# A decoder with two layers: one of three general PSUM banks becomes two halves for the attention units' transposed words, and four weights of the writing order change

## The chip, the core and the metric

The kernel is one program on one core of a Trainium2 chip. The metric is the device time of one execution in microseconds (us), from its start to its last store; less is better. Five engines take part, each working through its own list of instructions in order: PE (TensorE: matmuls and transposes, which write to PSUM), DVE (VectorE), ACT (ScalarE), POOL (GpSimd) and SP (which here issues most DMA transfers). Engines wait for each other by semaphores. An instruction that waits holds up everything behind it on its own engine.

## The reference, cut to what matters

The input x has 4 batches of 256 rows of 256 numbers, 1024 rows in all. Six blocks are added to it in turn, each on a layer norm of the rows: a linear attention with decay, four experts chosen by token, a layer that looks up 64 of 2048 small experts for each row, a convolution with attention inside blocks of 16 rows, a cross attention with quantised operands, and a layer of 16 experts of which each row uses two, beside a shared one. The change sits in the fifth block:

```
q = (x @ Wq + bq).reshape(1, B * N, H, hd)            # 1024 rows, 16 heads of 16
kv = (cond @ Wkv + bkv).reshape(1, -1, 2, H, hd)      # 1024 keys and values
q = _fq_sym(q, axis=-1); k = _fq_sym(k, axis=-1); v = _fq_sym(v, axis=2)
attn = jnp.einsum('bhqd,bhkd->bhqk', q, k)
attn = jax.nn.softmax(attn, axis=-1)
attn = _fq_unsigned(attn, axis=-1)                    # rounded to 255 steps of the row's maximum
out = jnp.einsum('bhqk,bhkd->bhqd', attn, v)          # then out @ Wp + bp
```

## The kernel before, in words

The 1024 rows are eight tiles (t = 0 to 7) of 128 rows. The cross attention is worked in 128 **units**, one for a tile and a head, by `units(k, n)` in six lanes. A unit does this:

1. PE writes the scores of 128 rows against 1024 keys into one of two score buffers, `sc0` and `sc1`, which are as large as two banks each (two matmuls `sc<-kT,qT`).
2. DVE takes the row's extreme from them (`junk<-sc,dsq,nsq`, result `nb`).
3. ACT takes the exponential, rounds it to bytes `e` and sums it; then the score buffer is given back.
4. PE transposes `e`, read as words of four bytes: two transposes `f<-ident,e` into half a PSUM bank `tp`.
5. ACT or DVE copies `tp` back over `e` (`e<-f`); then the bank is given back.
6. POOL turns the bytes into bf16 (`qqT<-e`), and PE multiplies them with the values in eight small matmuls into `accs`.

When the 16 heads of a tile are through, `cross_out` divides, transposes and projects them (`ident,ao`, `w_wp,aoT`) and adds them to the tile. `routes` then does the layer norm, the gate and the ranking of that tile, `shared` its shared expert. The tiles form two groups, 0 to 4 and 5 to 7. When a group's last tile is routed, `plan(g)` works out which rows each expert gets (its small matmuls are `ident_,ohs`). Then POOL fetches the rows of each expert tile from DRAM by an indirect DMA (`xr<-xs,smap`) and `routed` works on it: transposes `ident,xr`, two matmuls with the expert's weights (`w,xrT`), ACT and DVE, transposes `ident,rhd`, and two matmuls with `rhT`. Group 0 has 15 such tiles in two lanes beside the units (`beside`), group 1 has 12 in four lanes at the end (`ending`). `combine` fetches the results and adds them to the rows.

**PSUM.** `both`/`accs` takes one tile of 2 KB per partition, and seven more, `f0` to `f6`, are handed out by `bank`, an object of the class `Banks`: `take` gives the one that came free first, `give` returns it. Before the units begin, `turn` takes `f3` to `f6` out (`bank.leave(passed)`) and lays the two score buffers in their place, so that for the time of the units three general banks, `f0` to `f2`, are left. From these three come the words of all units and everything of `local_attention`, `cross_out`, `routes`, `shared`, `plan` and `routed`. When the last unit is done, `ending` closes the score buffers and gives four banks back.

**The order.** Nothing is scheduled by the tool: the order of instructions on each engine is the order in which the Python program writes them. Each strand of work is a generator that yields before each step, naming the engine that it needs next. `Clock.weave` keeps an estimated time for each engine (class `Clock`, `note`: a cost for each kind of instruction) and continues the strand that could start first, where each strand's start is moved ahead by its `lead` and ties go by its `rank`. So a lead, a rank or the number of free banks decides the order, and changes it everywhere behind. Every engine instruction is issued from one helper line, 81, so the rows of the profile are told apart by their tiles and not by their lines.

Of the kernel before, what the change touches and what calls it, by code (L numbers as in the profile page):

```python
# [21 lines left out]
P = 128  # L22
# [163 lines left out]
class Banks:  # L186
# [9 lines left out]
    def take(self, shape, dtype=F32):  # L196
        while not self.free:
            yield "tensor", self.ready()
        item = min(self.free, key=self.free.get)
        self.clock.t = max(self.clock.t, self.free.pop(item))  # L200
        pool, tag = item
        t = pool.tile(shape, dtype, name=tag.rstrip("0123456789"), tag=tag)
        self.held[id(t)] = item, t
        return t

# [39 lines left out]
def decoder(ctx, tc, a, out):  # L245
# [3 lines left out]
    ck = Clock(nc)  # L249
# [11 lines left out]
    A = SimpleNamespace(turned=None, scored=None, folded=None, cleared=[], spare=[], planned={}, mapped={}, loaded=None)  # L261
    wa = front_ctx.enter_context(tc.tile_pool(name="wa", bufs=1, side="right"))

    def load(pool, name, shape, view=None, dtype=F32):
        s = pool.tile(shape, dtype, name="w_" + name, tag="w_" + name)
        nc.sync.dma_start(s, a[name] if view is None else view)
        return s
# [30 lines left out]
    keys = load(wa, "keys", [P, 8, 2 * NKEY])  # L298
# [51 lines left out]
    psf = bank_ctx.enter_context(tc.tile_pool(name="psf", bufs=1, space=PSUM))  # L350
    kept, passed = [(psp, f"f{i}") for i in range(3)], [(psf, f"f{i}") for i in range(3, 7)]
    bank = Banks(ck, kept + passed)

    both = psp.tile([P, 2, D], F32, name="accs", tag="accs")
    accs = [both[:, i] for i in range(2)]
# [438 lines left out]
    def blend():  # L794

        for b in range(NB):
            yield "tensor", lambda: summed.get(("w", b))
            ww = wide["w", b]
            acc = yield from bank.several(2, [P, D])
            for i in range(2):  # L800
                for n in range(PN // 2):
                    te_.matmul(acc[i], ww[:, i, n, :], M.ut[:, n, :], start=(n == 0), stop=(n == PN // 2 - 1))
            summed["m", b] = ck.end
            yield "vector", None
            for i in range(2):
                t = 2 * b + i
                ve_.tensor_tensor(xt[t], acc[i], xt[t], ALU.add)
                bank.give(acc[i])
                added[t] = ck.end
            yield "vector", None  # L810
# [104 lines left out]
    def turn():  # L915
# [68 lines left out]
        mix_ctx.close()  # L984
        A.ps = score_ctx.enter_context(tc.tile_pool(name="ps", bufs=1, space=PSUM))
        A.sc = Banks(ck, [(A.ps, "sc0"), (A.ps, "sc1")])
        wd = late_ctx.enter_context(tc.tile_pool(name="wd", bufs=1))
        A.rt = late_ctx.enter_context(tc.tile_pool(name="rt", bufs=1))
        A.re = late_ctx.enter_context(tc.tile_pool(name="re", bufs=1))
# [193 lines left out]
    def units(k, n):  # L1183

        work = A.late
        for j in range(k, NT * XH, n):
            t, h = j // XH, j % XH
            yield "tensor", lambda: qready.get(t)
            o, c = h % 2, h // 2
            psc = yield from A.sc.take([P, T])  # L1190
            for n_ in range(2):
                te_.matmul(psc[:, n_ * 512:(n_ + 1) * 512], QT[t][:, o, c, :], KV.kT[:, c, n_ * 512:(n_ + 1) * 512],
                           start=True, stop=True)
            yield "vector", None
            nb = work.tile([P, 1], F32, name="nb", tag=f"nb{k}")
            ve_.tensor_tensor_reduce(A.junk, psc, DSQ[t][:, h:h + 1].to_broadcast([P, T]), NSQ[t][:, h:h + 1], 3.0e38,
                                     ALU.add, ALU.min, accum_out=nb)
            yield "scalar", None

            e = work.tile([P, T], U8, name="e", tag=f"e{k}")  # L1200
            se_.activation(e, psc, AF.Exp, bias=nb, scale=SQ[t][:, h:h + 1], accum_out=SUMS[t][:, h:h + 1])
            A.sc.give(psc)
            yield "tensor", None

            tp = yield from bank.take([P, 2, P])
            for o in range(2):
                te_.transpose(tp[:, o, :], e.bitcast(F32)[:, o * P:(o + 1) * P], ident)
            yield "either", None
            words = e.bitcast(I32).rearrange("p (o q) -> p o q", o=2)
            ck.leave(words, tp.bitcast(I32))  # L1210
            bank.give(tp)
            yield "gpsimd", None
            qqT = work.tile([P, 8, P], BF16, name="qqT", tag=f"qqT{k}")
            ge_.tensor_copy(qqT.rearrange("p (o j) q -> p o j q", o=2), words.bitcast(U8).rearrange("p o (q j) -> p o j q", j=4))

            yield "tensor", lambda: 0.0 if t < 2 else summed.get(("o", t - 2))
            for s in range(NT):
                te_.matmul(accs[t % 2][:, h * XD:(h + 1) * XD], qqT[:, s, :], KV.vi[:, s, h * XD:(h + 1) * XD],
                           start=False, stop=(s == NT - 1), skip_group_check=True)
            nunits[t] += 1  # L1220
            if nunits[t] == XH:
                summed[("x", t)] = ck.end
# [203 lines left out]
    def fetch_rows(g, i, xr):  # L1426

        ge_.indirect_dma_start(out=xr, out_offset=None, in_=xs[g],
                               in_offset=bass.IndirectOffsetOnAxis(ap=A.smap[g][:, i:i + 1], axis=0))
# [56 lines left out]
    def ending():  # L1486

        g = NG - 1
        yield "gpsimd", lambda: summed.get(("o", NT - 1))
        unit_ctx.close()  # L1490
        A.fin = fin_ctx.enter_context(tc.tile_pool(name="fin", bufs=1))
        score_ctx.close()
        pse = psum_ctx.enter_context(tc.tile_pool(name="pse", bufs=1, space=PSUM))
        for i in range(4):
            bank.free[pse, f"f{3 + i}"] = ck.end
        yield "gpsimd", lambda: A.mapped.get(g)
        got = {}

        def lane(k):
            for i in range(k, MOST[g], 4):  # L1500
                yield "tensor", lambda: got[i][1] if i in got else None
                yield from routed(g, i, A.fin, f"e{k}", *got[i])

        for i in range(MOST[g]):
            xr = A.fin.tile([P, D], F32, name="xr", tag=f"xre{i}")
            fetch_rows(g, i, xr)
            got[i] = xr, ck.end + 3.0
            if i < 4:
                ck.begin(lane(i))
            yield "gpsimd", None  # L1510
# [31 lines left out]
    def follow(b):  # L1542

        if b >= 2:
            yield "vector", lambda: known.get(b - 2)
        yield from front(b)

    def after_turn(gen, *args):
        yield "vector", lambda: A.scored
        yield from gen(*args)  # L1550

    with tc.manual_schedule(engines={mybir.EngineType.PE, mybir.EngineType.Activation, mybir.EngineType.DVE, mybir.EngineType.Pool}):
        lead = dict(front=(1.85, 0.2, 0.22, 0.3), begin=(0.0, 5.0, 10.0, 80.0), keys=1.2, dense=0.85,
                    blend=-0.82, mixing=(0.6, 0.53), local=(0.7, 0.6), units=0.66, out=0.77, shared=0.13,
                    route=0.66, ending=0.7, combine=0.3, routed=0.71, turn=0.1)
        rank = dict(front=(0, 9, 2, 4), keys=7, dense=1, blend=7, mixing=(5, 8), local=(7, 6), units=3,
                    out=4, routed=8, shared=9, route=2, turn=0, ending=2, combine=1)
        one = lambda k, i=None: (lead[k], rank[k]) if i is None else (lead[k][i], rank[k][i])
        ck.weave([*[Stream(follow(b), one("front", b), lead["begin"][b]) for b in range(NB)],
                  Stream(keys_values(), one("keys")), Stream(dense(), one("dense")), Stream(blend(), one("blend")),  # L1560
                  *[Stream(mixing(k, 2), one("mixing", k)) for k in range(2)],
                  Stream(tables(), one("turn")), Stream(turn(), one("turn")),
                  *[Stream(locals_(k), one("local", k)) for k in range(2)],
                  *[Stream(after_turn(units, k, UN), one("units")) for k in range(UN)],
                  Stream(cross_out(), one("out")), Stream(routes(), one("route")), Stream(shared(), one("shared")),
                  *[Stream(beside(k, 2), one("routed")) for k in range(2)],
                  Stream(ending(), one("ending")), Stream(combine(), one("combine"))])
# [6 lines left out]
    with tc.If(extra > 0, preferred_fallthrough_block=False):  # L1574
        for g, ts in enumerate(GROUPS):
            for i in range(MOST[g], NSL[g]):
# [4 lines left out]
                tp = ps.tile([P, 2, P], F32, name="tp", tag="tp")  # L1581
# [12 lines left out]
                tp = ps.tile([P, 2, P], F32, name="tp", tag="tp")  # L1594
# [18 lines left out]
            for i, t in enumerate(ts):  # L1613
                for j in range(2):
                    yg = work.tile([P, D], F32, name="yg", tag="yg")
                    nc.gpsimd.indirect_dma_start(
                        out=yg, out_offset=None, in_=ys[g],
# [83 lines left out]
```

## Time and profile before

| | us |
|---|---|
| three runs | 1013.13, 1009.01, 1011.62; median 1011.62 |
| the profiled execution | 1012.24 (its span 1010.5, so 1.7 lie around it) |
| before the units (0 to 577) | 577 |
| the units (577 to 913) | 336 |
| what follows the last unit (913 to the end) | 98 |

The three stretches are read from the times at which the first and the last unit's instructions start in the trace: the exponential of the first unit starts at 577.46, the last transposes of words at 911.45. Busy times of the whole span:

| engine | busy us | share |
|---|---|---|
| PE | 755.7 | 75% |
| DVE | 784.2 | 78% |
| ACT | 465.8 | 46% |
| POOL | 329.8 | 33% |

In rows of the profile "out<-in" are the tiles written and read, "x128" is a count, "idle before" is the time for which the engine stood still just before, and "<-" is what ended that. In a table by stage, each engine's busy time is followed by the number of its instructions, then come the granted PE clock, the busy share of the DMA engines and their GB/s.

### The profile page before, as it was taken

Reading aid. Unit: us, or ns where it says so; the run is one execution under the profiler, and the core shown is the slowest. Engines: PE = TensorE matmul, PEld = TensorE weight load, DVE = VectorE, ACT = ScalarE, POOL = GpSimd, SP = SyncE. Lnnn points to the kernel's source line nnn. Section 1 sums busy time; section 2 is a strip of 40 time slices with the busy share of each in tenths; the row PEclk is TensorE's granted clock in tenths of the full one; section 3 lists DMA queues with packets and bytes.
Section 4 is the critical chain, followed back from the end, with each engine's and each line's share of the span. In section 5 each row is a group of like instructions: output and inputs, shape, how many; then the busy total and the mean of one; then the engine's idle time right before and its main releaser. Section 6 shows DMA issues by size and latency. Waiting matters only on the chain.

```text
span 1010.5 us, 19521 instructions
## 1 busy us (share of the span) xinstructions
PE 755.7 (75%) x7395; PEld 572.9 (57%) x7430; DVE 784.2 (78%) x2121; ACT 465.8 (46%) x989; POOL 329.8 (33%) x298
## 2 busy tenths in 40 slices
PE   4587953879979798783888577876777768888693
PEld 3465652768768686773666454644455445554451
DVE  4668579898989897999677378889999788875343
ACT  2232440546226332430643177577768766753130
POOL 2000021351042304505511344334444445552522
PEclk9799995999979898796999889969898687999796
DMA  7000050000000001201000610000000290111323
GB/s 249 22 21 21 22 146 22 22 2 3 22 22 2 2 12 33 73 3 61 4 2 2 220 35 3 6 1 6 6 2 6 87 263 21 44 47 47 84 90 96
DMA packets 33938, 46.26 MB, mean 46 GB/s; under 512 B 6096, under 2 KB 25040, under 8 KB 33584
## 3 DMA queue, kind: packets, MB, share of 16 engines
q1 hardware_dynamic: 31776, 39.31, 12.6%
q0 software_dynamic: 2064, 5.64, 2.3%
q8 instruction: 61, 1.00, 0.4%
q14 instruction: 37, 0.30, 0.1%
HBM read 33.87 MB, written 11.08 MB: 44 GB/s over the span
## 4 chain that ended last, share of the span: by engine, by line
DVE 41%; PE 39%; ACT 8%; issue 6%; DMA 3%; POOL 1%; another core or an unknown queue 1%; SPq 0%; POOLq 0%; ACTq 0%; DVEq 0%
PE f L81 36%; DVE junk L81 7%; ACT e L81 5%; DVE aa L81 3%; PE sc L81 3%; DVE mi L81 2%; DVE rden L81 2%; DVE parts L81 2%; DVE jj L81 1%; DVE wq L81 1%; DVE at L81 1%; DVE oh L81 1%; DVE x L81 1%; DVE pk L81 1%; DVE f L81 1%
## 5 line engine op out<-in xcount | busy, mean ns | idle before, releaser
L81 POOL CAST qqT<-e 128x1024 bf16<-128x1024 uint8 x128 | 133.4, 1053 | 165.7 <-ACT e L81 129.6
L81 ACT ACTIVATE e<-sc,nb,qs_q 128x1024 uint8<-128x1024 f32 x128 | 153.9, 1203 | 47.3 <-DVE nb L81 44.2
L81 DVE CUSTOM_DVE_ANT_0 junk<-sc,dsq,nsq 128x1024 bf16<-128x1024 f32 x128 | 163.4, 1276 | 14.1 <-PE sc L81 5.8
L81 PE MATMUL sc<-kT,qT 128*128 128x512 bf16 x221 | 82.8, 449 | 68.3 <-ACT e L81 66.1
L81 POOL TENSOR_SCALAR at<-idx,row 128x512 f32<-128x512 uint8 x32 | 64.8, 2034 | 137.9 <-DMA idx<-mdram 100.7
L81 POOL TENSOR_TENSOR ln_rstd<-ln_ve,mhalf 128x2 f32<-128x2 f32 (+1 forms) x28 | 22.6, 807 | 198.9 <-DVE ln_ve L81 121.8
L81 PEld LDWEIGHTS <-qT 128*128 128x128 bf16 x256 | 23.9, 103 | 82.3 <-issue 78.4
L81 POOL TENSOR_TENSOR parts<-jj,wq 64x1024 f32<-64x1024 f32 x16 | 40.9, 2553 | 80.2 <-DVE wq L81 75.5
L81 PE MATMUL f<-ident,e 128*128 128x128 f32 x256 | 60.2, 323 | 8.1 <-ACT e L81 3.1
L81 PE MATMUL f<-zt,at 128*64 128x64 f32 x1024 | 46.1, 252 | 22.2 <-DVE at L81 19.9
L81 PEld LDWEIGHTS <-qqT 128*128 128x128 bf16 x1024 | 45.5, 101 | 23.5 <-issue 9.8
L81 PEld LDWEIGHTS f<-zt,at 128*64 128x64 f32 x1024 | 41.7, 163 | 29.6 <-issue 19.9
L81 ACT COPY ww<-f 64x256 f32<-64x256 f32 x128 | 46.9, 366 | 24.5 <-PE f L81 23.0
L81 PE MATMUL f<-w_ut,ww 128*128 128x256 f32 x256 | 56.0, 379 | 0.0
L81 PEld LDWEIGHTS f<-ident,e 128*128 128x128 f32 x256 | 37.5, 164 | 30.3 <-issue 10.3
L81 ACT ACTIVATE ln_xn<-x,ln_nmr,ln_rstd 128x256 f32<-128x256 f32 x48 | 27.0, 594 | 55.2 <-DVE ln_nmr L81 53.1
L81 PEld LDWEIGHTS f<-w_ut,ww 128*128 128x128 f32 x256 | 48.6, 190 | 6.6
L81 ACT COPY e<-f 128x256 int32<-128x256 int32 x106 | 38.7, 369 | 28.8 <-PE f L81 27.6
L81 PE MATMUL accs<-vi,qqT 128*128 128x16 bf16 x1024 | 45.5, 172 | 5.2 <-POOL qqT L81 3.3
L81 PE MATMUL f<-w,xrT 128*128 x108 | 40.1, 507 | 7.6 <-DVE xrT L81 7.0
L81 ACT COPY zt<-f 64x512 f32<-64x512 f32 x64 | 37.1, 580 | 18.3 <-PE f L81 17.4
L81 PE MATMUL f<-parts,aa 128*64 128x64 f32 x1024 | 36.6, 235 | 6.5 <-POOL parts L81 3.2
(317 smaller groups left out, 1823.8 us busy)
## 6 DMA issues: line engine op xcount, KB each, us to landing
w<-in_w SPq DMA_DIRECT2D x1, 5632.0 KB
idx<-mdram SPq DMA_DIRECT2D x32, 128.0 KB, 2.9
ys<-ryr SPq DMA_DIRECT2D x27, 128.0 KB, 1.7
kdram<-kb SPq DMA_DIRECT2D x4, 512.0 KB, 4.4
w_ut<-in_ut SPq DMA_DIRECT2D x2, 1024.0 KB, 11.8
kT<-kdram SPq DMA_DIRECT2D x8, 256.0 KB, 5.9
w_w2a<-in_w SPq DMA_DIRECT2D x1, 2048.0 KB, 26.9
ys<-zero SPq DMA_DIRECT2D x1, 1408.0 KB, 7.2
```

Of the source, the lines that this page charges most:

```text
L81: return emit(*args, **kw)
```

## The change

The half bank that a unit's words need no longer comes from the three general banks. `turn` takes one of them for good as `A.pair`, 128 partitions by 2 by 256 numbers, and makes its two halves the free items of a second `Banks` object, `half`. Units take and give halves, everything else has the other two banks. `ending` gives the pair back to `bank` once the last unit is through. Besides, three leads and a rank change: `out`, `routed` and `turn` (the lead of the strands `tables` and `turn`), and the rank of the units.

```diff
@@ Banks.take
-        t = pool.tile(shape, dtype, name=tag.rstrip("0123456789"), tag=tag)
+        if isinstance(tag, int):
+            t = self.tile[:, tag]
+            if len(shape) == 3:
+                t = t.rearrange("p (a b) -> p a b", b=shape[2])
+        else:
+            t = pool.tile(shape, dtype, name=tag.rstrip("0123456789"), tag=tag)
@@ decoder
     bank = Banks(ck, kept + passed)
+    half = Banks(ck, [])
@@ turn, after the score buffers are laid out
         A.sc = Banks(ck, [(A.ps, "sc0"), (A.ps, "sc1")])
+        A.pair = yield from bank.take([P, 2, 256])
+        for i in range(2):
+            half.free["half", i] = ck.end
+        half.tile = A.pair
@@ units
-            tp = yield from bank.take([P, 2, P])
+            tp = yield from half.take([P, 2, P])
...
-            bank.give(tp)
+            half.give(tp)
@@ ending
             bank.free[pse, f"f{3 + i}"] = ck.end
+        bank.give(A.pair)
@@ the weights
-                    blend=-0.82, mixing=(0.6, 0.53), local=(0.7, 0.6), units=0.66, out=0.77, shared=0.13,
-                    route=0.66, ending=0.7, combine=0.3, routed=0.71, turn=0.1)
-        rank = dict(front=(0, 9, 2, 4), keys=7, dense=1, blend=7, mixing=(5, 8), local=(7, 6), units=3,
+                    blend=-0.82, mixing=(0.6, 0.53), local=(0.7, 0.6), units=0.66, out=1.75, shared=0.13,
+                    route=0.66, ending=0.7, combine=0.3, routed=0.81, turn=-0.4)
+        rank = dict(front=(0, 9, 2, 4), keys=7, dense=1, blend=7, mixing=(5, 8), local=(7, 6), units=4,
```

Of the arithmetic nothing changes: every engine instruction is written as before, but on some of them ACT and DVE change places, since `Clock.leave` gives a copy out of PSUM to whichever of the two it reckons free first.

## The prediction

> **What bounds the kernel now.** I read the page first (the span, and busy shares of 75% for PE and 78% for DVE, so no engine bounds the whole), then a table by stage, and then, stage by stage, groups, waits and the order of time.
>
> ```profile
> span 1010.5 us, 19521 instructions
> ```
>
> ```profile
> core 0: us, PE busy (x) PEld busy (x) DVE busy (x) ACT busy (x) POOL busy (x), PEclk, DMA share, GB/s
> 470.00:577.00 107.00, 84.97 (x1187) 69.12 (x1189) 69.02 (x146) 38.97 (x89) 39.51 (x41) 0.93 0.14 44
> 577.00:913.00 336.00, 252.80 (x2259) 169.48 (x2292) 286.93 (x659) 234.72 (x476) 150.18 (x150) 0.86 0.15 44
> ...
> 913.00:980.00 67.00, 55.52 (x218) 33.03 (x217) 30.79 (x124) 17.86 (x60) 24.13 (x26) 0.90 0.29 78
> ```
>
> In the units' 336 us DVE is busy for 287, or 85%; ACT for 70%. Behind the last unit PE takes over (55.5 of 67 us). The groups and waits of the units' stage alone:
>
> ```profile
> L81 DVE CUSTOM_DVE_ANT_0 junk<-sc,dsq,nsq 128x1024 bf16<-128x1024 f32 x128 | 163.4, 1276 | 14.1 <-PE sc L81 5.8 <-remote 2.4 <-PE f L81 1.3
> L81 ACT ACTIVATE e<-sc,nb,qs_q 128x1024 uint8<-128x1024 f32 x128 | 153.9, 1203 | 47.3 <-DVE nb L81 44.2 <-DVE sw L81 0.5
> ...
> L81 PE MATMUL f<-ident,e 128*128 128x128 f32 x256 | 60.2, 323 | 8.1 <-ACT e L81 3.1 <-DVE qT L81 1.7 <-issue 1.2
> ...
> L81 ACT COPY e<-f 128x256 int32<-128x256 int32 x106 | 38.7, 369 | 28.8 <-PE f L81 27.6
> ...
> L81 DVE COPY e<-f 128x256 int32<-128x256 int32 x22 | 9.2, 420 | 0.9 <-PE f L81 0.9
> ```
>
> ```profile
> PE sc L81 <- ACT e L81: 66.1, 67, 9.3
> ACT e L81 <- DVE nb L81: 44.2, 53, 7.3
> ACT e L81 <- PE f L81: 27.6, 42, 1.7
> ```
>
> DVE's row maximum hardly waits (14.1 us over 128 units). ACT waits for DVE, and PE for ACT to free a score buffer. So the chain runs in turn over DVE, ACT and PE, with DVE the fullest. The third row of the groups is the one that the change is about: in front of all 256 transposes of words PE stood still for 8.1 us, and not all of that was for a bank.
>
> At the end the order of time shows what the last group waits for:
>
> ```profile
> 935.69 1.00 PE L81 MATMUL f<-ident__9641,ohs 128*128 128x42 bf16 x6 [1.03 <-DVE ohs L81]
> ```
>
> ```profile
> 938.47 0.95 POOL L81 DMA_INDIRECT xr<-xs,smap  x1 [10.00 <-DVE past L81]
> ```
>
> From the second plan's matmuls (935.69) to the first fetch of group 1's rows go 2.78 us. Twelve fetches follow, 1.26 us apart.
>
> **The change, part by part.** Durations are those of the profiled execution, 1012.24 us, so the sum is made against that.
>
> *What is removed.* I compared the waits written into both programs. Before, 48 waits of the units' first transposes are for an instruction that is no unit's (a copy, an addition, a `tanh` elsewhere) to empty its bank; after it, none. All that PE ever waited there is 8.1 us; of its parts named, 3.1 are for the exponential, which stays, and 1.7 for the copy of qT, a true bank holder. Bounds 0 and -8.1; I take **-2.0**, near the 1.7.
>
> *What the halves cost.* The program's waits do not know halves. Before, all 128 copies wait for their own unit's transposes. In the new order, 18 times the next unit's transposes are written ahead of this unit's copy (9 times before, then on another bank), and each of those 18 copies waits for the other unit's transposes as well. And 70 of the units' first transposes wait for another unit's copy, 33 before. So the pair works as one bank in turn. Throughput is not hurt: transposes and copy are 0.63 + 0.37 us, and a unit comes every 336/128 = 2.6 us. What is lost is an overlap: a copy that could run while the next transposes were on their way now comes after them, directly before the next copy, so one copy of 0.369 us stands on ACT's list each time, and behind it the exponential that frees a score buffer. 18 x 0.369 = 6.6 us at most, 0 at least; ACT is busy for 70% of the stage, so I take 70%: **+4.6**.
>
> [...]
>
> *What the other work pays.* It has two banks for three. In the stage, 122 tiles of it are taken before and 121 after. First writes that wait for a DVE instruction rise from 43 to 81; those that wait for a unit's copy fall from 46 to none. So some 38 waits change from an ACT copy of 0.37 to a DVE operation, 0.42 for most of them: 38 x 0.05 = **+1.9**. The upper bound is 38 x 0.42 = 16, if none of those waits existed before; below, 0.
>
> *What moves between ACT and DVE.* In the stage DVE loses six copies of words (6 x 0.42), a copy of `vo` (0.68), one of `xrT` (0.42), one `ryr` (0.42), a tile's layer norm and part of a shared expert (1.9), and gains ten `aoT` (10 x 0.352), two `kh` (0.95), a `vT` (0.45) and net one `rhT` (0.28): 5.2 less 5.9, or **-0.7**. Below, the six copies alone, -2.5; above, 0. ACT gets the reverse, and has room.
>
> *Before the units.* PE's list is the same to the first unit. On POOL a `parts` step goes ahead of five memsets; PE comes to `parts` only after its conv matmuls, so nothing is gained. On ACT the second strand's layer norm goes behind eight copies `ww` (3.03 us in all) and two `zt` (1.17), and its `xp` copy moves from DVE to ACT; the conv matmuls at 501.24, on the chain of waits, need it. Following the list of times: normed rows at 498.8 for 494.1, transposes at 499.4, two `qk` matmuls and a `qh` behind them, `xp` done at 502.1 where it was 501.1. **+0.9**, bounds -1 and +4.2.
>
> *Behind the last unit.* One route's gate and ranking and one shared expert's last matmuls come after the last unit that came before it: on PE two gate passes, ranking, `s2a` and `s2b`, less a pair of row transposes, 1.2 us by their rows. The second plan stands 7.4 us of PE work further behind the last unit's transposes than before (one expert tile's two matmul groups 1.45 + 1.30, two passes of `w_s` 2.90, small ones 1.75). That is work moved ahead of the plan, so behind it PE has less to cover the fetch: all 15 tiles of group 0 have been transposed, where one was left. What remains for PE there is the plan's 1.0, `rhd` and `hd` 0.83, `rhT` 1.30 and `s2` 1.2, 4.3 us; the first rows land 2.78 + 2.86 = 5.6 after the plan (2.86 is a fetch on the chain at 1001.46). PE stands still for 1.3 to 1.5. Together **+2.7**; 0 if other idle time swallows it, 7.4 if nothing behind the plan gets shorter.
>
> On SP's queue only stores change places; the three expert weight loads stand behind the same four stores of rows as before, so no transfer starts on another one's account.
>
> Sum: -2.0 + 4.6 + 1.9 - 0.7 + 0.9 + 2.7 = +7.4, so 1019.6; the profiled execution lies 0.6 above the median of the runs, so **1019**.
>
> **The rivals.** *The bank was the brake.* One mechanism: with a bank of its own no unit is held by local attention or a route, so PE's 8.1 us in front of the transposes go, and with them the exponentials that queue behind late copies. It decides from the point where the freed 8.1 is more than the false waits cost: if next transposes are seldom late, the 4.6 is 0. Then -8.1 - 2.5 (the six copies less on DVE's full list) + 1.9 + 0.9 + 2.7 = -5.1, and 0.6 to the median: **1007**. For it: the 48 waits, and that ACT's longest waits are for DVE. Against: 27.6 us over 42 waits, 0.66 each, for copies is just the length of two transposes (0.63), so copies follow promptly already.
>
> *DVE hides it all.* DVE's work in the stage changes by -0.7 and 85% of it is busy, so waits of PE and ACT pass behind it; the plan's delay passes into PE's 6 us standstill at 950 to 956. Then **1012**. Against: 49 us of the stage DVE does stand still.
>
> *Two banks are too few.* The 16 us above come in full, as DVE is the engine that empties them and is the fullest: 1019 + 14 = **1033**. Against: the order was written with two banks in mind, as late takes show (routes' gates come behind units 32, 51 and 71, for 27, 47 and 62).
>
> **How the numbers follow.** Forecast 1019 (its own range 1013 to 1027) has 0.42, the freed bank 0.33, DVE hides it 0.17, too few banks 0.08. About 0.5%, 5 us, is what a measurement of this kernel can tell from no change. Faster: the freed bank, 0.33. Slower: too few banks and most of the forecast, 0.45. Same: the rest, 0.22. The range takes in the freed bank down to 1002, and the upper bounds up to 1033; a tenth on either side is left.
>
> **What would show it.** The halves: exponentials' waits for PE `f` above 27.6 us, with PE's idle time before `f<-ident,e` no lower than 8.1. The banks: PE `f` waiting longer for DVE. The end: the second plan's `ohs` at some 30 us behind the last unit's transposes instead of 24 (935.69 less 911.45), and a wait for rows after it. Before the units: the first exponential at 578.4 for 577.46. If the units' stage is shorter than 330 us, the freed bank was right and I was wrong; if the end comes later by more than 7 us, the plan was priced too low.

## The result, and the profile after

The changed kernel takes 1023.75 us (median of seven runs, 1019.16 to 1033.45); the kernel before took 1012.42 beside it (1009.01 to 1015.2). The ratio is 1.0131, with a 95% interval of 1.0105 to 1.0156. A second series, with a profile of its own, gave 1.0128 (1.0093 to 1.0162). So the change costs 11 us by the medians and 13 by the ratio, where the prediction's sum was 7.4.

The profiled execution took 1026.25 us. Its span, and the stretches between the first unit's exponential, the last unit's transposes, the second plan's matmuls and the end:

```profile
span 1024.3 us, 19507 instructions
```

```profile
core 0: us, PE busy (x) PEld busy (x) DVE busy (x) ACT busy (x) POOL busy (x), PEclk, DMA share, GB/s
577.50:916.30 338.80, 250.56 (x2236) 167.46 (x2269) 290.36 (x646) 230.25 (x464) 148.20 (x149) 0.85 0.14 42
916.30:947.40 31.10, 26.51 (x123) 16.49 (x121) 17.55 (x83) 10.59 (x37) 6.84 (x8) 0.95 0.16 51
947.40:1024.30 76.90, 54.16 (x172) 30.40 (x172) 27.36 (x89) 13.20 (x43) 27.28 (x28) 0.74 0.30 85
```

The same three stretches in the second profile of the same program:

```profile
574.20:913.60 339.40, 252.91 (x2235) 169.48 (x2268) 289.34 (x645) 230.14 (x464) 148.30 (x149) 0.84 0.14 43
913.60:944.80 31.20, 26.59 (x123) 16.56 (x123) 17.57 (x83) 10.61 (x37) 6.93 (x8) 0.95 0.16 51
944.80:1018.20 73.40, 47.61 (x172) 27.59 (x172) 27.31 (x89) 13.25 (x43) 27.31 (x28) 0.80 0.32 89
```

The same three in the kernel before:

```profile
577.50:911.60 334.10, 251.50 (x2254) 168.84 (x2288) 285.74 (x655) 234.03 (x474) 149.69 (x149) 0.86 0.14 44
911.60:935.70 24.10, 19.56 (x90) 11.50 (x89) 14.03 (x64) 7.67 (x27) 5.46 (x6) 1.00 0.18 54
935.70:1010.50 74.80, 50.80 (x186) 29.81 (x186) 28.67 (x96) 14.75 (x48) 26.80 (x28) 0.81 0.32 90
```

So the units' stage is 5 us longer and the second plan stands 7 us further behind it, in both executions. What lies behind the plan is 2.1 us longer in one and 1.4 shorter in the other: the two differ by 3.5 us there with the same instructions, of which more below. What precedes the first exponential (577.5, 574.2; 577.5 before) scatters by 3 us and shows nothing.

The groups of the units' stage, and its waits:

```profile
L81 DVE CUSTOM_DVE_ANT_0 junk<-sc,dsq,nsq 128x1024 bf16<-128x1024 f32 x127 | 162.3, 1278 | 15.1 <-PE sc L81 7.3 <-PE f L81 0.9 <-DVE nb L81 0.8
L81 ACT ACTIVATE e<-sc,nb,qs_q 128x1024 uint8<-128x1024 f32 x128 | 154.1, 1205 | 50.9 <-DVE nb L81 45.7 <-DVE count L81 2.7
...
L81 PE MATMUL f<-ident,e 128*128 128x128 f32 x256 | 58.8, 318 | 6.7 <-ACT e L81 5.4 <-issue 0.7
...
L81 ACT COPY e<-f 128x256 int32<-128x256 int32 x111 | 40.1, 369 | 37.7 <-PE f L81 34.2 <-DVE e L81 1.1 <-DVE rhd L81 0.8
...
L81 DVE TENSOR_SCALAR aoT<-f,sv 128x128 f32<-128x128 f32 x13 | 4.0, 347 | 2.9 <-PE f L81 2.7
```

```profile
PE sc L81 <- ACT e L81: 65.6, 65, 9.6
ACT e L81 <- DVE nb L81: 46.0, 46, 7.6
ACT e L81 <- PE f L81: 34.2, 42, 2.0
```

Of the two signs that the prediction named for the halves, the first seems to be there: ACT's copies wait for PE for 34.2 us where it was 27.6. The second, at least 8.1 us of PE's idle time in front of the transposes, is not: PE loses 6.7, of which 5.4 are for the exponential (3.1 before). The plan, as forecast, stands 31 us behind the last transposes:

```profile
947.41 1.01 PE L81 MATMUL f<-ident__9541,ohs 128*128 128x42 bf16 x6 [1.26 <-DVE ohs L81]
```

The experiments show that the copies' longer waits have another cause than the halves.

### The profile page after: what moved, and what is told of

The parts are those of the page before. It is cut to its first block, busy times and chain, and to the rows that moved or that the text cites. A ratio compares the mean times of both kernels' runs of the same rounds, so it can differ in the third digit from the quotient of the medians.

```text
span 1024.3 us, 19507 instructions
## 1 busy us (share of the span) xinstructions
PE 764.6 (75%) x7396; PEld 576.6 (56%) x7430; DVE 790.7 (77%) x2124; ACT 464.0 (45%) x986; POOL 327.7 (32%) x298
## 5 line engine op out<-in xcount | busy, mean ns | idle before, releaser
L81 PE MATMUL sc<-kT,qT 128*128 128x512 bf16 x222 | 80.5, 437 | 67.9 <-ACT e L81 65.6
L81 PEld LDWEIGHTS f<-zt,at 128*64 128x64 f32 x1024 | 41.7, 163 | 29.5 <-issue 20.2
L81 PE MATMUL f<-w,xrT 128*128 x108 | 42.5, 528 | 5.8 <-issue 3.6
```

The source lines that it names most:

```text
L81: return emit(*args, **kw)
```

## The experiments

The change does two things at once: it divides the banks otherwise, and it writes the work in another order. To take them apart, the order was made a constant. `weave` was run once for each of the two kernels, and the strand that it continued at each step was noted, and for each copy out of PSUM whether it went to ACT or DVE. These lists, some 2,800 steps each, were then written into the kernel. A step whose bank is not free is put off until it is, and nothing else moves.

```diff
@@ Clock.weave
-        while live:
...
-            _, t, s = min(able, key=lambda x: (x[0] - x[2].lead, x[2].rank, x[1]))
+        for name in PLAN["picks"]:
+            s = known[name]
...
+                    while s.todo and step(s):
+                        s.todo -= 1
@@ Clock.leave
-        if max(now, self.free["scalar"]) + 0.2 + n * 0.00083 <= max(now, self.free["vector"]) + 0.15 + n * 0.00104:
+        if PLAN['left'][self.now.id][self.now.left - 1] == "1":
```

"Old" and "new order" below are these two lists, "three banks" is the `Banks` object of before, "halves" that of the change. The computation is the same in all of them. In the tables, "stage" runs from the first exponential to the last unit's transposes, "to plan" from there to the second plan's matmuls, "behind" from there to the end, each from the profile of that kernel.

**The banks, with the order held.**

*e1: new order, three banks.* Every engine's list is the changed kernel's.

> Every engine's list is the changed kernel's, instruction for instruction; only the banks differ: units' transposes and other work share three whole banks, as before the change. If the halves and the two remaining banks cost what the prediction says (4.6 + 1.9 - 2.0), the time falls by 4.5 us from the changed kernel's, to a ratio of about 1.0085, with the units' stage (first exponential to last unit's transposes) 334 us instead of 338.8 and the exponentials' waits for PE back from 34.2 to about 28 us; the second plan stays 31 us behind the last transposes. If the loss is all in the order of the work, ratio 1.013 and the stage 338.8. If it is all in the banks, 1.000 to 1.003.

*e2: old order, halves.* At 82 of its 2,803 steps something is put off because no bank is free.

> The order of the kernel before, with the halves of the changed kernel; where a third bank for other work was in use at once, the step is put off until one of the two is free, and nothing else moves. Banks at the prediction's price: 4.5 us more than before, ratio 1.004 to 1.005, units' stage 338 us, the second plan 24 us behind the last transposes and the stretch behind it as before. Loss all in the order: 1.000. Loss all in the banks: 1.013, stage 345 us or more.

*e4: new order, the pair as one whole bank for one unit at a time.*

```diff
-        for i in range(2):
-            half.free["half", i] = ck.end
+        half.free["half", 0] = ck.end
```

> The changed kernel's order with the pair as one bank for one unit at a time: at the places where a unit's transposes stood ahead of the last unit's copy (18 by their order) they go right behind it, nothing else moves. If the copies' waits for the other unit's transposes cost the 4.6 us of the prediction, they come back: ratio 1.0085, exponentials' waits for PE about 28 us instead of 34.2. If they are hidden, 1.013. If transposes that start later hold up PE, 1.015 or more.

*e5: the changed kernel again.*

> The changed kernel once more, unaltered, beside the kernels that are compared with it. Ratio 1.011 to 1.016. If the new order with three whole banks (1.018) is really slower than with the halves, this stays below 1.0165. The tail behind the last unit's transposes again near 108 us where the kernel before has 99; if that was the clock of one execution, it comes out at 102 or less this time.

| kernel | ratio (95%) | stage | to plan | behind |
|---|---|---|---|---|
| before | 1 | 334.1 | 24.1 | 74.8 |
| the change | 1.0131 (1.0105 to 1.0156) | 338.8 | 31.1 | 76.9 |
| e5, the same | 1.0128 (1.0093 to 1.0162) | 339.4 | 31.2 | 73.4 |
| e1 new order, three banks | 1.0178 (1.0154 to 1.0202) | 341.4 | 30.5 | 72.3 |
| e4 new order, one bank | 1.0206 (1.0182 to 1.0231) | 346.0 | 29.6 | 76.0 |
| e2 old order, halves | 1.0284 (1.0259 to 1.0309) | 356.0 | 28.9 | 72.4 |

The rows of words in the units' stage, of e1 (first two) and e4 (last two):

```profile
L117 PE MATMUL f<-ident,e 128*128 128x128 f32 x255 | 58.9, 319 | 4.1 <-ACT e L117 3.1 <-DVE pr L117 0.3 <-DVE qT L117 0.3
...
L117 ACT COPY e<-f 128x256 int32<-128x256 int32 x111 | 40.3, 369 | 34.3 <-PE f L117 33.4 <-ACT hT L117 0.2
```

```profile
L117 PE MATMUL f<-ident,e 128*128 128x128 f32 x256 | 61.8, 330 | 10.9 <-ACT e L117 9.1 <-DVE e L117 1.3
...
L117 ACT COPY e<-f 128x256 int32<-128x256 int32 x111 | 40.9, 368 | 48.2 <-PE f L117 47.1 <-ACT e L117 0.6 <-issue 0.2
```

In the change none of the 128 copies runs while transposes write into the pair; in e1, with whole banks, 23 copies run beside transposes of words, and 17 in the kernel before. So the overlap that the prediction saw lost is indeed gone. Three things follow all the same. With the new order, giving the three banks back does not return the 4.5 us that the prediction put on the halves; the kernel is slower still, 1.0178 for 1.013. The intervals of the two just touch, and the stage is 1.0 to 2.6 us longer in e1 and in e11 below, which has the same stage. So the halves may gain up to 5 us, and they cost nothing. The copies wait 33.4 us for PE with three banks as well: that sign belongs to the order. And e4 shows that the halves are not "one bank in turn", as the prediction had it. When the next transposes really have to wait for the copy, the stage grows by 6.6 to 7.2 us and the copies' waits to 47.1. Writing the next unit's words into the other half ahead of the copy is an overlap that pays, though the copy then has to wait until those transposes are done.

In the old order the halves cost 28 us, 22 of them in the stage:

```profile
576.30:932.30 356.00, 264.02 (x2288) 172.12 (x2288) 285.46 (x656) 234.37 (x474) 150.61 (x149) 0.85 0.14 41
```

DVE does the 285 us of work that it did before and stands still for 70 us of 356, where it was 48 of 334. Its waits for PE's `f` rise from 14.8 to 30.2 us, and some 12 of these 15 us stand in front of other work than the units'; PE's idle time in front of the units' own transposes is 6.0 us, not more than before. So the two remaining banks are too few for the old order, which was written for three, and the new order is what makes them suffice. It has its own price, and the next question is where.

**The order, with three banks held.** Here the two lists are joined: one order up to a point, then whatever is left in the other order.

*e9: new order up to the first unit, then the old.*

> Three whole banks; the new order up to the first unit, the old order from there on. The prediction's term for this part is 0.9 us: ratio 1.001. If a good part of the new order's 18 us (1.018 with three banks) comes from here, 1.005 or more, with the first exponential later than 580 us.

*e10: old order up to the last unit, then the new.*

> Three whole banks; the old order up to the last unit, and what is left then in the new order: 69 matmuls instead of 61 between the last unit's transposes and the second plan, 268 behind it. The prediction's term is 2.7 us, ratio 1.0027. If the tail's order makes the 9 us that the changed kernel loses there, 1.009.

*e11: new order up to the last unit, then the old.*

> Three whole banks; the new order up to the last unit, and what is left then in the old order: 77 matmuls ahead of the second plan and 276 behind it (old order throughout: 61 and 276). If what the units' stage leaves undone makes the loss, this stays at 1.015 to 1.018, with 6 us or more of it behind the last transposes though the order there is the old one. If the tail's order makes it, 1.007 to 1.010.

*e12: the kernel before with nothing but the four changed weights*, so that `weave` finds an order for three banks itself.

```diff
-                    blend=-0.82, mixing=(0.6, 0.53), local=(0.7, 0.6), units=0.66, out=0.77, shared=0.13,
-                    route=0.66, ending=0.7, combine=0.3, routed=0.71, turn=0.1)
+                    blend=-0.82, mixing=(0.6, 0.53), local=(0.7, 0.6), units=0.66, out=1.75, shared=0.13,
+                    route=0.66, ending=0.7, combine=0.3, routed=0.81, turn=-0.4)
```

(and the rank of the units, 4 for 3).

> The kernel before with the changed weights of the writing order and its own three shared banks; the order that follows from them is another one than the changed kernel's: the first plan comes at unit 127 instead of 105. The weights alone: if they are good by themselves, 1.000 or less; if the first plan's late place pushes group 0's experts behind the units, 1.02 or more.

| kernel | ratio (95%) | stage | to plan | behind |
|---|---|---|---|---|
| e9 new up to the units | 1.0011 (0.9998 to 1.0023) | 334.9 | 25.6 | 73.9 |
| e10 new behind the units | 1.0051 (1.0026 to 1.0076) | 334.2 | 28.2 | 74.5 |
| e11 new up to the last unit | 1.0167 (1.0145 to 1.0188) | 340.4 | 31.4 | 74.6 |
| e12 new weights, own order | 1.0404 (1.0377 to 1.0430) | 340.2 | 41.7 | 95.5 |

The part before the units costs nothing that can be told from no change, and the order behind them 5 us. The loss is in e11. These are e9's rows for the stage and the stretch to the plan, and e11's (its tail is in the old order):

```profile
575.10:910.00 334.90, 255.12 (x2288) 168.34 (x2288) 286.15 (x654) 234.22 (x474) 150.19 (x149) 0.85 0.14 44
910.00:935.60 25.60, 20.91 (x89) 12.41 (x89) 14.10 (x64) 7.71 (x27) 5.46 (x6) 0.93 0.16 51
```

```profile
575.80:916.20 340.40, 260.71 (x2269) 171.66 (x2269) 287.31 (x645) 229.63 (x464) 148.22 (x148) 0.83 0.14 42
916.20:947.60 31.40, 25.17 (x110) 15.20 (x109) 16.61 (x77) 9.61 (x33) 7.09 (x8) 0.84 0.15 46
947.60:1022.20 74.60, 50.57 (x186) 29.85 (x186) 28.61 (x96) 14.71 (x48) 26.76 (x28) 0.80 0.31 90
```

The stage is 5.5 us longer than in e9 and leaves more undone: 77 matmuls stand between the last transposes and the plan, where it is 61 in the old order, and this stretch takes 31.4 us for 25.6. PE is busy for 4.3 us more in it, at a granted clock of 0.84 for 0.93, so a part of this can be the clock. The parts don't add up (1.0167 and 0.0051 are more than the 1.0178 of e1), so a few us belong to neither alone. e12 says that the weights are nothing by themselves: with three banks they lead to an order in which the first plan comes at unit 127 instead of 105, and 40 us are lost.

**Where in the stage.** Three more kernels join the orders inside the stage, with three banks.

*e13: new order to unit 108, then the old.*

> Three whole banks; the new order up to unit 108 of 128 (first plan included), the old order from there: 61 matmuls between the last unit's transposes and the second plan. If the stage up to and with the first plan makes the loss, 1.010 or more. If the late route and the shared experts of the last 20 units make it, this is back at 1.003 to 1.006, of which 4 us are the stretch around the first plan.

*e14: old order to unit 108, then the new.*

> Three whole banks; the old order up to unit 108, the new one from there: the route of tile 5 at unit 126, 85 matmuls ahead of the second plan. If the last 20 units' order makes the loss, 1.010 to 1.014, the second plan some 31 us behind the last transposes and the first plan's stretch as in the kernel before. If not, 1.005, which is the tail's order alone.

*e15: new order to unit 66, then the old.*

> Three whole banks; the new order up to unit 66, the old from there. At unit 64 the new order is 5 us ahead, with 9 us less of DVE's other work behind it. If that half costs anything, 1.004 or more; otherwise 1.000 to 1.003.

They gave 1.0230 (1.0205 to 1.0254), 1.0142 (1.0120 to 1.0163) and 1.0121 (1.0095 to 1.0148), and they settle nothing. e14's exponentials follow those of the kernel before to within 0.1 us up to unit 108 and lose 11.9 us within the next four units; e15's lose 15.7 against e9's in the twelve units from 64 on, around its joint. What one order had done by then and the other had not comes all at once at the joint and holds up the units. That joint costs as much as what was to be located. (e9 to e11 have theirs where no units wait.)

The times of the exponentials, counted from the first one, are what remains; they are from the profiles of e9 (the old order in the stage), e11 and e5:

| unit | 28 | 32 | 64 | 84 | 104 | 108 | 127 |
|---|---|---|---|---|---|---|---|
| e9, old order, three banks | 80.4 | 90.6 | 170.7 | 212.8 | 265.4 | 275.6 | 332.1 |
| e11, new order, three banks | 79.7 | 95.3 | 165.9 | 219.4 | 267.9 | 282.5 | 338.9 |
| e5, the change | 80.0 | 95.2 | 166.6 | 218.2 | 266.9 | 282.1 | 338.0 |

The new order is 5 us behind at unit 32, 4 to 5 ahead at 64, 5 to 7 behind at 84 and 1.5 to 2.5 behind at 104: other work comes at other times. From 104 to 108, around the first plan, it loses 4.3 to 5.0 us. One instruction stands out there. These are DVE's, POOL's and ACT's rows at the first plan in the changed kernel, and below them DVE's in the kernel before:

```profile
848.85 3.22 DVE L81 TENSOR_SCALAR te<-tef 128x25 int32<-128x25 f32 x1
849.04 3.00 POOL L81 CAST qqT<-e 128x1024 bf16<-128x1024 uint8 x3
...
853.37 1.20 ACT L81 ACTIVATE e<-sc,nb,qs_q 128x1024 uint8<-128x1024 f32 x1 [2.71 <-DVE count L81]
```

```profile
844.46 0.18 DVE L81 TENSOR_SCALAR te<-tef 128x25 int32<-128x25 f32 x1
```

A conversion of 25 numbers takes 3.22 us, where it took 0.18, until three conversions of words on POOL are through; the row maximum behind it waits, and ACT's exponential after that.

*e16: this instruction taken out of the changed kernel, order and halves as they are.*

```diff
-        ve_.tensor_reduce(tef, past, AX.X, ALU.add)
-        ve_.tensor_scalar(A.te[g], tef, float(NE - 1), None, ALU.min)
+        ve_.tensor_reduce(tef, past[:, :, 0:NE - 1], AX.X, ALU.add)
+        se_.copy(A.te[g], tef)
```

> The changed kernel, order and halves as they are, but the expert numbers of the plan are limited by summing 15 experts instead of 16 and converted on ACT: DVE's instruction of 3.2 us at the first plan is gone. If it held up the units, 3 us come back: 1.010. If the next DVE instruction stands still in its place, 1.013.

1.0115 (1.0081 to 1.0149): not to be told from the changed kernel's 1.0128, which was measured on another chip. In its profile the four units around the plan take 14.1 us instead of 15.2, so about one of the three us comes back there. But DVE then waits elsewhere: it is busy for 287.1 us of the stage and stands still for 55.7, where it was 290.4 and 48.4, and the stage is 342.8 us long.

**Which engine copies.** *e17: the changed kernel with the old placement of its copies; e18: the kernel before with the new placement.* The list of `leave` above is exchanged for the other kernel's, the order of steps is not.

> The changed kernel's halves and order of steps, but each copy out of PSUM on the engine that had it before the change (ten aoT back to ACT, seven copies of words to DVE, two kh and others). If DVE's new copies, which wait for PE in line with the row maxima, make the stage's loss, 1.005 to 1.008 and DVE's idle time in the stage 8 us less. If placement is worth the prediction's -0.7, 1.013 to 1.014.

> The kernel before, order of steps and banks as they are, with the changed kernel's placement of the copies on ACT and DVE. By the prediction's term 0.999; if the placement makes the loss, 1.005 to 1.008. A placement that does not fit the order of its steps may cost in both kernels: then both are slower than their own, and the placement alone explains nothing.

e17 gave 1.0239 (1.0216 to 1.0262) and e18 1.0097 (1.0067 to 1.0127). Each order is slower with the other's placement, by about 1%, so the placement alone is not what makes the new order slow. 99 copies change engines, 51 one way and 48 the other, and cost 10 us where they don't fit the steps around them.

**The second plan's place.** *e3: in the changed kernel the last output, the last two routes and the plan get a lead of 6; e6: the shared experts of tiles 4 and 5 too; e7: the same in the kernel before; e8: in the changed kernel, only these two shared experts, with a lead of 3.*

```diff
@@ cross_out
             yield "vector", lambda: summed.get(("x", t))
+            if t == NT - 1:
+                ck.now.lead = 6.0
@@ routes
+            if t >= 6:
+                ck.now.lead = 6.0
             yield from route(t)
@@ shared (e6 and e7; 3.0 in e8)
         for t in range(NT):
+            ck.now.lead = 6.0 if 4 <= t <= 5 else 0.13
```

> The changed kernel, but behind the last unit the last cross-attention output, the last two routes and the second plan are taken before experts and shared experts; the order up to there is the same. PE has 59 matmuls instead of 85 between the last unit's transposes and the plan, so the plan should stand about 22 us behind them instead of 31. If the end follows the plan's place, 7 to 9 us come back, ratio 1.004 to 1.006. If PE's work alone bounds the end (what is put off has to be done behind the plan), nothing changes: 1.012 to 1.014. If the loss in the tail is a lower granted clock, the time follows the clock of the run and not the plan's place.

> The changed kernel, with the shared experts of tiles 4 and 5 taken ahead as well, since a route starts only when the shared expert two tiles before has begun: the last route no longer waits for it, and only 31 matmuls stand between the last unit's transposes and the second plan (85 in the changed kernel). The plan should stand 18 to 22 us behind the transposes. If the end follows the plan's place, 9 us come back: 1.004 to 1.006. If PE's work bounds the tail, the end stays: 1.013. If filler is then missing ahead of the plan, PE stands still there and the end is later: 1.016 or more.

> The kernel before with the same treatment of its tail: 23 matmuls instead of 61 between the last unit's transposes and the second plan. If the end follows the plan's place, 5 us or more below the kernel before, ratio 0.993 to 0.996. If PE's work bounds the tail, 1.000; if PE stands still ahead of the plan, 1.003 or more.

> The changed kernel with nothing but the shared experts of tiles 4 and 5 taken earlier: 53 matmuls between the last unit's transposes and the plan, near the 61 of the kernel before. If the late shared expert, by way of the last route, is what the tail's 9 us are, about 6 of them come back: 1.006 to 1.008. Otherwise 1.013.

| kernel | ratio (95%) | stage | to plan | behind | matmuls behind the plan |
|---|---|---|---|---|---|
| e3 | 1.0201 (1.0175 to 1.0227) | 339.6 | 30.8 | 78.6 | 142 |
| e6 | 1.0317 (1.0285 to 1.0348) | 359.9 | 17.5 | 86.2 | 148 |
| e8 | 1.0210 (1.0176 to 1.0243) | 351.2 | 20.5 | 82.1 | 118 |
| e7 (kernel before) | 1.0148 (1.0117 to 1.0179) | 347.9 | 16.6 | 86.3 | 150 |

From the plan's own matmuls on, the changed kernel runs 116 matmuls and the one before 124. (The 268 and 276 of the expectations above take in 152 more in a branch for expert tiles beyond the fixed number, `tc.If(extra > 0)`, of which no trace has a row.) All four are slower than what they came from. In e3 the plan did not move, though 26 matmuls fewer stood before it. Its order of time shows why (`x<-f,x`, with which the last tile is ready for its route, was done at 927.6):

```profile
935.26 0.23 DVE L81 TENSOR_SCALAR gsel<-gsel,ws 128x2 f32<-128x2 f32 x1
935.40 0.42 DVE L81 BATCH_NORM_STATS2 ln_st<-x 128x6 f32<-128x256 f32 x1
...
935.41 1.45 PE L81 MATMUL f<-w_s,xnT 128*128 128x352 f32 x4
...
937.82 0.44 PE L81 MATMUL f<-ident,ln_xn 128*128 128x128 f32 x2 [0.96 <-ACT ln_xn L81]
```

`routes` starts a tile only when the shared expert two tiles before has begun (`t - 2 not in doing`), since its normed rows have two buffers. So the norm of the last tile (`ln_st`) is written right behind the start of tile 5's shared expert (`gsel`, `w_s`), 7.8 us after that tile was ready. What holds the plan is the shared experts' lag, and not the matmuls around it. e6 to e8 lift that lag, but the work that goes ahead then stands before the last units: the stage grows by 12 to 21 us. And what is put off has to be done behind the plan, in e3, e6 and e7; in e8, with 118 matmuls there, PE is busy for only 51.5 of 82.1 us, and why it stands still longer was not followed. This leaves no gain, and none of the kernels tried is faster than the one before.

## Why the prediction was wrong, though it had the direction

It had the direction, and a sum of 7.4 us against 11.3 by the medians (13 by the ratio). Most of its terms were wrong: the halves were priced too dear and the order too cheap. That the sum came as near as it did is luck.

- *Before the units, +0.9:* e9 fits it (1.0011, 1.1 us) but can't be told from nothing, and the first exponential, which was to come 0.9 us later, scatters by 3.
- *Removed waits, halves and two banks, together +4.5:* wrong. In the order of the change the halves cost nothing and may gain up to 5 us (e1 against the change). The copies' waits of 34.2 us, named as their sign, are there with three banks too. The waits were read rightly; the error is in "the pair works as one bank in turn" and in the price of these waits: e4 made it one bank in turn, and it costs 7 us of stage more than the halves do. That these waits cost what an overlap is worth was an estimate, and it is wrong; no run leaves the waits out, so what the halves would do without them is not shown. What the halves do cost was to be seen only in an order made for three banks: 28 us (e2), which is the rival "two banks are too few" at nearly twice its bound of 16. The new order avoids that.
- *What moves between ACT and DVE in the stage, -0.7:* **this is the step that failed.** It priced the new order by the instructions that change sides and by nothing else. With the banks held, the new order in the units' stage costs some 16 us (1.0167 less 0.0011). In the profiles some 6 of them are in the stage itself and 6 in front of the second plan, where it leaves 16 matmuls more. DVE's busy time in the stage is 1.2 us (e11) to 4.2 us (the change) above e9's and not 0.7 below it.
- *Behind the last unit, +2.7:* too small, within its bounds. Its 7.4 us for the plan's place came true (31.1 and 31.2 us for 24.1). But most of it was put down to the tail's order; e11, with the old order there, has the same 31.4, so what the stage leaves undone is enough for it. (The tail's order alone gives 28.2, in e10.) And the relief behind the plan, which took the 7.4 down to 2.7, hardly came: 73.4 and 76.9 us for 74.8, with 8 matmuls fewer. On a chip on which nothing else stops PE there (see below), 8 matmuls fewer make this stretch 1.1 to 1.5 us shorter (64.7 and 64.4 us in e14 and e16, 65.8 and 65.9 in e13 and e15); in the change a standstill of 3.6 to 7.0 us and the clock can cover that. The order of the tail alone costs 5 us (e10).
- *The rivals:* "The bank was the brake" fell as a forecast, though its mechanism, the overlap of a bank of its own, was nearer to the truth than the term that was put against it. What was held against it, that a copy's wait of 0.66 us is the length of two transposes, is loose: a pair takes 0.63 us or more in some 30% of the units of the kernel before, 0.38 to 0.44 in nearly all others and 0.48 on the mean. "DVE hides it all" fell: DVE's idle time in the stage is 48 to 50 us as before, its busy time is 3.6 to 4.6 us longer, and that is most of the 5 us by which the stage grew.

What stays open is which steps of the new order cost the 6 us within the stage. The four units around the first plan hold 4 to 5 of them, and the conversion beside POOL is one part of that, about 1 us by e16, which the stage as a whole did not gain. The rest wasn't located.

## What to carry to other kernels

Where a planner writes the order, a resource and the order that was found for it are one thing: taken alone, the halves cost 28 us, the new weights 40, and the new order with the old banks 18, while the three together cost 13. So an order cannot be priced by counting what moves in it; ask what is left undone when the fullest stage ends, since that comes again in front of the next thing that everything waits for. Holding the recorded order and exchanging the resource is a cheap way to tell the two apart, as long as no joint of two orders lies inside a stage where work queues.

## What the runs showed of the hardware

**A slow clock under full load.** Granted PE clock behind the plan in the changed kernel, in two stretches of 10 us each:

```profile
967.40:977.00 9.60, 8.92 (x20) 4.69 (x21) 2.07 (x8) 2.06 (x8) 1.91 (x3) 0.50 0.22 65
977.00:987.00 10.00, 9.83 (x26) 5.32 (x25) 2.10 (x7) 2.46 (x8) 0.00 (x0) 0.62 0.09 31
```

PE is busy for 96% of the time from 967.4 to 984.5 and gets half its clock (0.50) all the while, 17.1 us. From 970.8 on PE has no gap, so half the clock goes on for 13.7 us of work without one. Two `w_w2a` matmuls take 1.22 us there and 0.60 from 989 on. PE had stood still for 3.6 us before 967.4. After such a restart the kernel before has its clock back in 4.9 us (956.0 to 960.9) and e5 in 3.2 (968.4 to 971.6); in e5 this stretch at half clock lasts 6.8 us and not 17.1. The same 172 matmul records behind the plan took 54.16 us in this execution of the change and 47.61 in e5. What decides how long the half clock lasts is not shown.

**A standstill on some chips.** About 15 us behind the second plan, PE, DVE and ACT stop in the kernel before, for something that the trace doesn't name (`remote`):

```profile
955.53 0.76 DVE L81 COPY xrT<-f 128x256 f32<-128x256 f32 x2 [6.03 <-remote]
...
956.01 6.23 PE L81 MATMUL f<-w,xrT 128*128 x12 [6.02 <-DVE xrT L81]
```

It is there in e9, the change, e5 and e11 too (5.3, 3.6, 7.0 and 6.0 us on PE). Waits that end by `remote` stand in this stretch in every profile but those of e13 to e18. These six ran on two other chips; there they are missing, and the stretch behind the plan takes 62.9 to 65.9 us instead of 72 to 77 in kernels with the same tails. The kernel before took 1003.58 and 1000.51 us on those chips. What the standstill is stays open. The ratios of e1 to e18 each compare runs on one chip, but the change itself was run only on chips with the standstill, so e13 to e18 are held against a ratio from elsewhere.

**Small DVE instructions took longer beside POOL.** The 3.22 us of `te<-tef` (0.18 in the kernel before) are the longest case; it began 0.2 us before the first of three conversions of 1.0 us each on POOL and lasted until the third was through. In the units' stage of the kernel before some 26 DVE instructions took at least 0.15 us more than the shortest of their kind, about 16 us in all, and nearly all of that time belongs to those that overlap an instruction on POOL, which is busy for 150 of the 334 us. In the changed kernel there are some 27 with about 20 us. What holds these up is not shown: in the stage of the kernel before some 310 of the 655 DVE instructions overlap one on POOL, and all but those 26 or so stay within 0.15 us of the shortest of their kind.
